# Two layers of graph attention on one core: in the sets of v product 6 goes ahead of product 3, and a block sum of features moves from VectorE to GpSimd

## The chip, the core and the metric

The kernel runs on one core of a Trainium2 chip. The metric is the device time of one execution in microseconds (us). Before the change three runs took 3329.23 to 3331.56 us, with a median of 3330.91 us.

The core has five engines that run their own instruction streams and wait for each other through semaphores: TensorE (PE in the profile; its weight loads are shown as PEld), VectorE (DVE), ScalarE (ACT), GpSimd (POOL) and SyncE (SP), which here only starts transfers.

## The reference

There are 4096 nodes with 512 features and an adjacency matrix of 4096 x 4096. Layer 0 is graph attention with 4 heads of 128, layer 1 is masked attention with 8 heads of 64; each is added to its input and normalised.

```python
x = _layernorm(x + _L0_gnn_ref(x, adj, ...), axis=-1)
x = _layernorm(x + _L1_gnn_ref(x, adj, Wks, Wqs, Wvs, Wo), axis=-1)

# in _L1_gnn_ref
adj = jnp.maximum(adjacency_matrix, eye)
q = jnp.einsum('nd,hdk->hnk', node_matrix, Wqs)
k = jnp.einsum('nd,hdk->hnk', node_matrix, Wks)
v = jnp.einsum('nd,hdk->hnk', node_matrix, Wvs)
scores = jnp.einsum('hqk,hmk->hqm', q, k) * kd ** (-0.5)
scores = scores + IDENTITY_BIAS * eye - MASK_VAL * (1.0 - adj)
att = jax.nn.softmax(scores, axis=-1)
return jnp.einsum('hqm,hmk,hko->qo', att, v, Wo)
```

The change lies in the three lines that make q, k and v: three matrix products of 4096 x 512 by 512 x 512, in float32.

## The kernel before

The program has four stages, one behind the other: the projections of layer 0 (to about 216 us of the span), its attention (to 1126 us), the projections q, k and v of layer 1 (to about 1412 us), and the attention of layer 1 with the output projection (to the end). The order of instructions on each engine is the order in which the Python code issues them.

**A set.** The features are taken in four pairs of 512-row groups (pair 0 to 3), that is 1024 rows at a time. For each pair `gemm` is called three times, for k, q and v: a set. A set treats the features (1024 x 512) and the weights (512 x 512) as two matrices of 2 x 2 blocks and makes the four blocks of the result, "11", "12", "21" and "22", from seven block products instead of eight. Products 1, 2, 3 and so on are numbered in the code; some of their factors are plain blocks, others are sums of blocks, made beforehand by `combine_weights` for weights and `combine_features` for features. The results follow from

- "11" = product 1 + product 2
- u2 = product 1 + product 6, and "12" = u2 + product 5 + product 3
- u2 becomes u2 + product 7, and "21" = u2 + product 4, "22" = u2 + product 5

The tile `u2` holds the running sum (two buffers), and `p5` holds product 5 (one buffer). An add with an operand in PSUM is on VectorE (`add`, L1283); the two adds of p5 read SBUF only and are on GpSimd (`pool`, L1277): first p5 into "12", called out12 below, later u2 + p5 into "22", called out22. Each finished block goes to device memory in two transfers on SyncE's queue (L1268, L1273). The text that follows uses the short names of the profile: v_sb and k_sb are the tiles for results, since `take_out` borrows them.

**Small sets.** From pair 1 on, some products are themselves made of seven small products of quarter size: products 1, 5, 6 and 7 in the k and q sets, products 1 and 5 in the v sets. `begin` issues four of them, `end` the other three (L1294 for v, L1298 for k and q), and a full product of something else stands between, so that VectorE and ScalarE have time to empty PSUM. These "deep" sets are issued by `in_parts` from a list, `plan`. A pair (1, 0) in it is the begin of product 1, (1, 1) its end, a plain number a whole product (L1248 for v, L1255 for k and q). The v set of pair 0 and the v set of pair 3 have no small sets and follow the older order 1, 5, 2, 6, 7, 3, 4; only the v sets of pairs 1 and 2 take the part of the list that the change edits. For brevity "(6, 0)" is also called the small set 6.

**PSUM.** `new` takes a tile of the pool of three s_ps tiles (1024 columns), `spread` takes both x_ps tiles (512 columns each), of which there are no more. In a deep v set products 2 and 3 are spread, and 1, 5, 6, 4 and 7 take new tiles in turn. A product can only start when the tile that it takes has been read.

**Sums for the next pair.** While a v set runs, the sums of features that the next pair needs are made: on VectorE four block sums of 128 x 1024 (`combine_features`, L1224) into the tiles x_s (products 5, 6 and 4) and in place (7), and on GpSimd quarter sums of 128 x 256, four for each small set 1, 5, 6 and 7 (`combine_features2`, L1214), into the tiles x2_s. They depend on each other: block sum 6 is made from 5, block sum 4 from 6, and the quarter sums of 5, 6 and 7 from the block sum of the same number. The tiles bear the name adjT in the profile, or xT for the sum in place. `beside_at(n, fn, ...)` puts such a step behind product n of the set: it is issued there, on its engine, behind the adds of that product.

Of the kernel before, what the change touches and what calls it, by code (L numbers as in the profile page):

```python
# [429 lines left out]
def tile_gat_then_masked_attention(  # L430
# [16 lines left out]
    nc = tc.nc  # L447
# [119 lines left out]
    with tc.tile_pool(name="l0", bufs=NG) as l0, \  # L567
# [77 lines left out]
        with tc.tile_pool(name="l0s", bufs=2) as sp:  # L645
# [264 lines left out]
            for g in range(NG):  # L910
                fs[g] = l0.tile([P, 2, GT, H0], F32, name="f")
                s4 = sp.tile([P, H0, GT, W0], F32, name="s4")
                plan = end if g == NG - 1 else usual if g else begin
# [60 lines left out]
        def turn_x1(g, n, c):  # L974
            nc.vector.transpose(
                xTs[g][:, c, n * HG:(n + 1) * HG].rearrange("p (b r) -> p b r", r=SQ),
                ys[g, n][:, :, c * SQ:(c + 1) * SQ])
# [119 lines left out]
    with wait_by_tile("l1", 1) as l1, wait_by_tile("l1a", 2) as lp, \  # L1097
# [46 lines left out]
        with wait_by_tile("l1s", 2) as sp:  # L1144
# [84 lines left out]
            def gemm(w, sums, kind, pair, beside, deep=()):  # L1229
# [7 lines left out]
                def new():  # L1237
                    return [ps.tile([P, HP, G], F32, name="s_ps").rearrange("p e r -> p (e r)")]
# [25 lines left out]
                def store(c, queue=nc.sync):  # L1264
                    for n in range(2):
                        m, g = 2 * (int(c[0]) - 1) + n, 2 * pair + int(c[1]) - 1
                        if kind == "v":
                            queue.dma_start(  # L1268
                                v_d[m][g // 2][:, g % 2 * GT:(g % 2 + 1) * GT, :],
                                out[c].rearrange("p (t d) -> p t d", t=GT)[  # L1270
                                    :, :, n * P:(n + 1) * P])
                        else:
                            queue.dma_start(k_d[m][g // 2][:, g % 2, :] if kind == "k"  # L1273
                                              else q_d[m][g], out[c][:, n * G:(n + 1) * G])

                def pool(dst, a, c, op):
                    nc.gpsimd.tensor_tensor(dst, a, c, op=op)  # L1277

                def add(dst, t):
                    n = 2 * G // len(t)  # L1280
                    for k, src in enumerate(t):
                        at = slice(k * n, (k + 1) * n)
                        nc.vector.tensor_tensor(dst[:, at], src, u2[:, at], op=ALU.add)  # L1283

                def spread():
                    return [xp.tile([P, GT, P], F32, name="x_ps").rearrange("p t r -> p (t r)")
                            for _ in range(2)]
# [66 lines left out]
                def results(i):  # L1354

                    if i == 1:
                        add(out["11"], held.pop(2))
                        store("11")
                    elif i == 6:
                        add(out["12"], held.pop(3))  # L1360
                        pool(out["12"], out["12"], p5, ALU.add)
                        later.at(1, lambda: store("12"))
                    elif i == 7:
                        pool(out["22"], u2, p5, ALU.add)
                        add(out["21"], held.pop(4))
                        store("21")
                        later.at(1, lambda: store("22"))

                def in_parts():
                    plan = [(1, 0), (5, 0), 2, (1, 1), (5, 1)]  # L1370
                    plan += [(6, 0), 3, (6, 1), (7, 0), 4, (7, 1)] if 6 in deep else [3, 6, 4, 7]
                    for i in plan:
                        if isinstance(i, int):
                            t = new() if i in (4, 6, 7) else spread()
                            product(i, t)
                            if i in (6, 7):
                                add(u2, t)
                                results(i)
                            else:
                                held[i] = t  # L1380
                        else:
                            i, phase = i
                            if phase == 0:
                                begin(i, p5 if i == 5 else u2, i in (1, 5))
                                continue
                            end(i)
                            results(i)
                        for fn in beside.get(i, []):
                            fn()
                        later.step()  # L1390

                if deep:
                    in_parts()
                    return
# [41 lines left out]
            for pair in range(NG // 2):  # L1436
                more = pair + 1 < NG // 2
                halves = [(2 * pair + 2 + n // 2, n % 2) for n in range(4)] if more else []

                def bring(n):  # L1440
                    load_x1(*halves[n], turn_p if pair % 2 else sp)

                def turn(n):
                    for c in range(KC):
                        turn_x1(*halves[n], c)

                beside = {}

                def beside_at(n, fn, *args):
                    beside.setdefault(n, []).append(lambda: fn(*args))  # L1450

                def parts(kind):
                    return inner[kind] if pair and (more or kind != "v") else ()

                if pair == 0:
                    combine_features(nc.vector, 0, 5)
                    for n, i in ((1, 6), (5, 7), (2, 3)):
                        beside_at(n, combine_weights, nc.vector, wk, wk_s, i)
                    for n, i in ((1, 6), (5, 7), (2, 4)):
                        beside_at(n, combine_features, nc.vector, 0, i)  # L1460
                    for i, n in ((5, 7), (6, 7), (7, 3), (3, 4)):
                        beside_at(n, combine_weights, nc.gpsimd, wq, wq_s, i)
                    beside_at(4, load_all, wv, wvs)
                elif pair == 1:
                    for n, i in ((2, 1), (5, 5), (3, 6), (4, 7)):
                        beside_at(n, combine_weights2, nc.vector, "q", wq, wq_s, i)
                if more:
                    for k, n in ((5, 0), (7, 1)):
                        beside_at(k, bring, n)
                gemm(wk, wk_s, "k", pair, beside, parts("k"))  # L1470
                beside = {}
                if pair == 0:
                    for i, n in ((5, 5), (6, 2), (7, 6), (3, 7)):
                        beside_at(n, combine_weights, nc.gpsimd, wv, wv_s, i)
                elif pair == 1:
                    for n, i in ((2, 1), (3, 5)):
                        beside_at(n, combine_weights2, nc.gpsimd, "v", wv, wv_s, i)
                if more:
                    for k, fn, n in (((2, turn, 0), (2, bring, 2), (4, turn, 1), (4, bring, 3),
                                      (7, turn, 2)) if pair else  # L1480
                                     ((1, turn, 0), (5, turn, 1), (5, bring, 2), (6, bring, 3),
                                      (4, turn, 2))):
                        beside_at(k, fn, n)
                else:
                    load_adjT(0, 0)
                    load_q(0, 0)
                gemm(wq, wq_s, "q", pair, beside, parts("q"))
                beside = {}
                if more:
                    beside_at(2 if pair else 1, turn, 3)  # L1490
                    if pair == 0:
                        for n, i in ((2, 1), (6, 5), (7, 6), (3, 7)):
                            beside_at(n, combine_weights2, nc.vector, "k", wk, wk_s, i)
                    for i, n in ((5, 5), (6, 6), (7, 3 if pair else 2), (4, 4)):
                        beside_at(n, combine_features, nc.vector, pair + 1, i)
                    for i, n in (((1, 1), (5, 6), (6, 4), (7, 7)) if pair else
                                 ((1, 1), (5, 6), (6, 3), (7, 4))):
                        beside_at(n, combine_features2, nc.gpsimd, pair + 1, i)
                else:
                    beside_at(5, load_kv, 0, 0, 0)  # L1500
                    beside_at(2, load_adjT, 0, 1)
                    for t in range(GT):
                        beside_at(2, finish_md, 0, t)
                    beside_at(7, load_kv, 0, 0, 1)
                    for c in range(2, NCJ):
                        beside_at(3, load_adjT, 0, c)
                gemm(wv, wv_s, "v", pair, beside, parts("v"))
                xTs.pop(2 * pair)
                xTs.pop(2 * pair + 1)
# [280 lines left out]
```

## Time and profile before

| what | us |
| --- | --- |
| median of three runs | 3330.91 |
| the profiled execution | 3330.41 |
| its span | 3328.3 |
| TensorE busy | 3301.2 |
| VectorE busy | 2484.2 |
| GpSimd busy | 2167.3 |
| v set of pair 1, first matmul to first matmul of the next set | 24.56 |
| v set of pair 2, the same | 24.56 |

The span runs from the first instruction to the last of the profiled execution; its own time is longer by what lies around it. The page gives the busy time of each engine. A wait is given as the idle time of an engine and what ended it: "<-DVE p L1311" means that an instruction of line 1311 on VectorE, writing p, did. In timelines a row is a group of equal instructions with its start, its length, the engine, the line, the tiles out<-in, the shape and the count. One matmul of the code can be two rows' worth of records (a product of eight matmuls is "x16" in the v sets). In the table by stage each row has the stretch, its length, and the busy times of the engines in the order PE, PEld, DVE, ACT and POOL, each with its count, then the clock of TensorE as a share, the share of the transfer engines and GB/s.

### The profile page before, as it was taken

The page shows a single profiled execution, that of the slowest core. Times are in us where ns is not written, and L with a number is a line of the kernel's source. Part 1 is how long each engine was busy: PE and PEld are TensorE (multiplying, and loading weights), DVE is VectorE, ACT ScalarE, POOL GpSimd, SP SyncE. Part 2 cuts the span into 40 slices and gives each one's busy share as a digit, 9 for nine tenths or more (in the row PEclk, how much of TensorE's full clock was granted, in tenths as well). Part 3 has the DMA queues.
Part 4 walks back from the last instruction along what each step waited for, and adds up shares of the span by engine and source line. Part 5 has one row for each costly group of instructions (what it writes and reads, how often), then busy time and mean ns, then how long its engine had stood idle before and what let it go on. Part 6 is the DMA issues. An engine that isn't in the chain of part 4 may idle for free.

```text
span 3328.3 us, 67210 instructions
## 1 busy us (share of the span) xinstructions
PE 3301.2 (99%) x27160; PEld 1965.5 (59%) x27160; DVE 2484.2 (75%) x3189; ACT 1949.1 (59%) x2439; POOL 2167.3 (65%) x1599
## 2 busy tenths in 40 slices
PE   9999999999999999999999999999999999999998
PEld 8899999999999777733333333333333333333333
DVE  6789899899999676567767676676766767667676
ACT  1267868878776310156656556566565656656554
POOL 5630040040030243389999999999999999999996
PEclk9999999999999999999999999999999999999999
DMA  8988796686532443489888988879888799887984
GB/s 180 227 204 183 219 187 169 152 184 146 137 93 58 111 149 114 149 223 205 191 211 226 224 202 191 210 188 257 203 194 212 186 214 244 194 210 186 213 196 112
DMA packets 398992, 612.04 MB, mean 184 GB/s; under 512 B 167632, under 2 KB 248528, under 8 KB 398672
## 3 DMA queue, kind: packets, MB, share of 16 engines
q0 software_dynamic: 97520, 258.77, 42.6%
q1 hardware_dynamic: 299280, 345.88, 33.5%
q8 instruction: 215, 3.52, 0.4%
q10 hardware_dynamic: 1872, 3.02, 0.4%
q14 instruction: 105, 0.86, 0.1%
HBM read 315.87 MB, written 109.25 MB: 128 GB/s over the span
## 4 chain that ended last, share of the span: by engine, by line
PE 92%; POOL 3%; DMA 2%; DVE 1%; issue 1%; ACT 0%; ACTq 0%; POOLq 0%; DVEq 0%
PE o_ps L1087 27%; PE o_ps L1597 24%; PE s_ps L1138 24%; PE o_ps L846 5%; PE s_ps L1661 3%; PE s_ps L1298 2%; PE s_ps L1255 2%; DMA p<-p 2%; PE s_ps L1248 1%; PE x_ps L1255 1%; POOL q_sum L1572 1%; PE x_ps L1248 1%; PE s_ps L1616 1%; POOL p L1582 0%; POOL adjT L1214 0%
## 5 line engine op out<-in xcount | busy, mean ns | idle before, releaser
L1572 POOL TENSOR_TENSOR q_sum<-q_sum,p 128x1024 f32<-128x1024 f32 x538 | 1378.0, 2561 | 64.0 <-DMA p<-p 38.2
L1552 DVE TENSOR_TENSOR p<-s_ps,adjT 128x1024 f32<-128x1024 f32 x896 | 1043.9, 1217 | 470.1 <-ACT s_ps L1549 438.4
L1549 ACT ACTIVATE s_ps<-s_ps 128x1024 f32<-128x1024 f32 x1021 | 967.5, 1006 | 597.3 <-PE s_ps L1138 594.2
L1138 PE MATMUL s_ps<-q_sb,k_sb 64*64 64x512 f32 x8192 | 943.5, 589 | 2.8 <-DVE p L1552 2.7
L1597 PE MATMUL o_ps<-p,v_sb 64*64 64x512 f32 x8192 | 943.6, 590 | 0.0
L1087 PE MATMUL o_ps<-sup_t,p 128*128 128x129 f32 x8192 | 915.7, 275 | 1.2 <-DVE p L640 1.2
L1087 PEld LDWEIGHTS o_ps<-sup_t,p 128*128 128x128 f32 x8192 | 915.3, 192 | 1.7 <-DVE p L640 1.4
L640 DVE SCALAR_TENSOR_TENSOR p<-fr_t,dj,az 128x1024 f32<-128x1024 f32 x512 | 650.2, 1284 | 66.1 <-PE o_ps L1087 37.9
L1138 PEld LDWEIGHTS s_ps<-q_sb,k_sb 64*64 64x64 f32 x8192 | 312.4, 133 | 569.9 <-issue 453.7
L1597 PEld LDWEIGHTS o_ps<-p,v_sb 64*64 64x64 f32 x8192 | 310.2, 133 | 570.7 <-issue 560.4
L624 ACT ACTIVATE z<-fr_t,f 128x1024 fp8e4<-128x1024 f32 x512 | 557.9, 1146 | 102.1 <-DVE az L635 101.8
L1582 POOL DMA_DIRECT2D p<-p x412 | 438.4, 1302 | 10.1 <-PE o_ps L1597 9.2
L1063 POOL DMA_DIRECT2D agg<-base_d x32 | 29.1, 1217 | 386.8 <-DMA sup_t<-sup_d 204.7
L585 POOL COPY seen<-token 128x1 f32<-128x1 f32 x24 | 10.9, 455 | 356.8 <-DVE token L583 356.8
L1552 DVE TENSOR_TENSOR p<-s_ps,md 128x1024 f32<-128x1024 f32 x128 | 150.8, 1218 | 67.0 <-ACT s_ps L1549 63.6
L635 DVE TENSOR_TENSOR az<-adjT,z 128x512 int32<-128x512 int32 x256 | 175.4, 685 | 2.9 <-ACT z L624 1.8
L600 ACT ACTIVATE adjT<-stage 128x1024 fp8e4<-128x1024 bf16 x128 | 131.2, 1055 | 17.0 <-DMA stage<-adj_d 16.7
L1661 PE MATMUL s_ps<-wo_sb,on 128*128 128x512 f32 x240 | 110.8, 604 | 0.0
L1631 ACT ACTIVATE r<-r_h 32x256 f32<-32x256 f32 x248 | 102.3, 413 | 2.9
L1277 POOL TENSOR_TENSOR v_sb<-v_sb,p 128x1024 f32<-128x1024 f32 x8 | 20.6, 2569 | 95.9 <-DVE v_sb L1283 52.4
L1049 ACT ACTIVATE agg<-o_ps,rinv 128x128 f32<-128x128 f32 x128 | 42.0, 370 | 69.8 <-DVE den L1042 45.9
L1322 ACT ACTIVATE v<-s_ps 128x256 f32<-128x256 f32 x28 | 10.8, 384 | 117.6 <-PE s_ps L1298 102.5
(274 smaller groups left out, 2257.3 us busy)
## 6 DMA issues: line engine op xcount, KB each, us to landing
p<-p POOLq DMA_DIRECT2D x412, 512.0 KB, 9.1
k_sb<-k_d SPq DMA_DIRECT2D x128, 512.0 KB
v_sb<-v_d SPq DMA_DIRECT2D x128, 512.0 KB
adj_d<-in_adj_dram POOLq DMA_DIRECT2D x32, 1024.0 KB, 11.0
sup_t<-sup_d SPq DMA_DIRECT2D x120, 258.0 KB
fr_t<-fr_d SPq DMA_DIRECT2D x16, 1024.0 KB
adjT_d<-adjT SPq DMA_DIRECT2D x32, 512.0 KB
adjT<-adjT_d SPq DMA_DIRECT2D x32, 512.0 KB
```

The lines of the kernel that those rows point to most:

```text
L624: nc.scalar.activation(z[:, k, :], fr_t[w, h][:, 0, :], AF.Sign, bias=fs[j // GT][:, 0, (j + k) % GT, h:h + 1], saturate=False)
L635: nc.vector.tensor_tensor(az.bitcast(I32), adjT[w, j // CJ][:, j % CJ:j % CJ + 2, :].bitcast(I32), z.bitcast(I32), op=ALU.bitwise_and)
L640: nc.vector.scalar_tensor_tensor(p, fr[:, 1, :], dj[j // GT][:, j % GT, h:h + 1], az_t[w, h, j // 2][:, j % 2, :], op0=ALU.max, op1=ALU.mult)
L846: nc.tensor.matmul(out[:, t * HD:(t + 1) * HD], xb[:, c, t * P:(t + 1) * P], wb[:, c, :], start=not more and t == 0 and c == 0, stop=c == ...
L1087: nc.tensor.matmul(o[t // BK][:, t % BK, :], p[:, t * P:(t + 1) * P], s, start=(j == 0 and t % BK == 0), stop=(j == NT - 1), skip_group_ch ...
L1138: nc.tensor.matmul(s[c:c + MS, e, :], k[r, a + c:a + c + MS], qt[g, m][r, :], start=True, stop=True)
L1549: nc.scalar.activation(s, s, AF.Exp, scale=float(KD) ** -0.5)
L1552: nc.vector.tensor_tensor(p, s, keep[:, None, :].to_broadcast([P, HP, G]), op=ALU.mult)
L1572: nc.gpsimd.tensor_tensor(q, q, p, op=ALU.add)
L1582: later.at(2, lambda: nc.gpsimd.dma_start(a, b, accum_op=ALU.add))
L1597: nc.tensor.matmul(o[c, n, :], v[r, j % CH, c], p[r, e, :], start=(j == 0), stop=(j == NT - 1))
L1661: nc.tensor.matmul(s, on_t[g][:, m, t * P:(t + 1) * P], wo_sb[:, m, :], start=(m == 0), stop=(m == NP1 - 1))
```

## The change

Three edits. First, in the deep v sets (pairs 1 and 2) product 6 is issued ahead of product 3; the adds for "12" now stand behind product 3, and those for "21" and "22" behind product 7, as before. Second, GpSimd's quarter sums are ordered anew: in the v set of pair 0 those of 7 ahead of those of 6; in the v sets of pairs 1 and 2 those of 7 come behind product 3 and those of 6 behind product 7, where before they stood the other way round behind products 4 and 7. With that GpSimd has the quarter sums of 5 ahead of out12, and those of 7 between out12 and out22; those of 6 follow out22. Third, block sum 4 (128 x 1024) is no longer issued on VectorE behind product 4 but on GpSimd, as its last step of the set.

On VectorE the block sum of 7 comes behind the adds of "12" now, because product 3 is later in the list.

```diff
                 def in_parts():
                     plan = [(1, 0), (5, 0), 2, (1, 1), (5, 1)]
-                    plan += [(6, 0), 3, (6, 1), (7, 0), 4, (7, 1)] if 6 in deep else [3, 6, 4, 7]
+                    plan += [(6, 0), 3, (6, 1), (7, 0), 4, (7, 1)] if 6 in deep else [6, 3, 4, 7]
                     for i in plan:
                         if isinstance(i, int):
                             t = new() if i in (4, 6, 7) else spread()
                             product(i, t)
                             if i in (6, 7):
                                 add(u2, t)
-                                results(i)
                             else:
                                 held[i] = t
+                            if i == 7 or i == 3 and 6 not in deep:
+                                results(2 * i if i == 3 else i)
...
-                    for i, n in ((5, 5), (6, 6), (7, 3 if pair else 2), (4, 4)):
+                    for i, n in ((5, 5), (6, 6), (7, 3 if pair else 2)):
                         beside_at(n, combine_features, nc.vector, pair + 1, i)
-                    for i, n in (((1, 1), (5, 6), (6, 4), (7, 7)) if pair else
-                                 ((1, 1), (5, 6), (6, 3), (7, 4))):
+                    for i, n in (((1, 1), (5, 6), (7, 3), (6, 7)) if pair else
+                                 ((1, 1), (5, 6), (7, 7), (6, 4))):
                         beside_at(n, combine_features2, nc.gpsimd, pair + 1, i)
+                    beside_at(7 if pair else 4, combine_features, nc.gpsimd, pair + 1, 4)
```

## The prediction

> **What bounds the kernel now.** I read the page first, then the list of what TensorE waited for, then the chain that ended last around the sets of v, then the timelines there.
>
> The page:
>
> ```profile
> span 3328.3 us, 67210 instructions
> ...
> PE 3301.2 (99%) x27160; PEld 1965.5 (59%) x27160; DVE 2484.2 (75%) x3189; ACT 1949.1 (59%) x2439; POOL 2167.3 (65%) x1599
> ...
> PE 92%; POOL 3%; DMA 2%; DVE 1%; issue 1%; ACT 0%; ACTq 0%; POOLq 0%; DVEq 0%
> ```
>
> TensorE is busy for 99% and carries 92% of the chain. Work that leaves VectorE or GpSimd is worth only what TensorE waits for it. The list of TensorE's waits (total us, times, longest) has two rows from the sets that the change edits:
>
> ```profile
> PE s_ps L1138 <- DVE p L1552: 2.7, 3, 1.8
> PE s_ps L1298 <- DVE p L1311: 1.8, 2, 0.9
> PE x_ps L1248 <- DVE v_sb L1283: 1.6, 2, 0.8
> ```
>
> The lower two come once in the v set of each of the second and third pairs of feature blocks, and in the k set behind it. TensorE's timeline around the first (start, length, in brackets the idle time before):
>
> ```profile
> 1252.67 0.61 PE L1294 MATMUL s_ps<-wv_s,adjT 128*128 128x128 f32 x4
> 1254.08 3.69 PE L1248 MATMUL x_ps<-adjT,xT 128*128 128x256 f32 x16 [0.80 <-DVE v_sb L1283]
> 1257.61 3.62 PE L1248 MATMUL s_ps<-wv_s,adjT 128*128 128x256 f32 x16
> ...
> 1275.72 0.59 PE L1298 MATMUL s_ps<-adjT,wk 128*128 128x256 f32 x2
> 1277.23 0.67 PE L1298 MATMUL s_ps<-adjT,wk_low 128*128 128x256 f32 x2 [0.92 <-DVE p L1311]
> ```
>
> At 1254.08 product 3 waits: it writes the two x_ps tiles that held product 2, and VectorE empties them until 1254.53. At 1277.23, in the next k set, the end of small set 5 waits for VectorE's p, which waits for GpSimd. The chain names what GpSimd did:
>
> ```profile
> 1263.94 3.20 POOL v_sb L1277
> 1267.14 1.67 POOL adjT L1214
> ...
> 1273.85 2.32 POOL k_sb L1277
> 1276.17 0.02 issue
> 1276.20 0.44 DVE p L1311
> ```
>
> Between out12 (v_sb, from 1263.94) and out22 (k_sb, from 1273.81) stand eight quarter sums of the next pair's features (L1214). p5 has one buffer, so the k set can't write it until out22 has read it. Both engines were slow beside each other here; two of VectorE's block sums (L1224) and one quarter sum, from the two engines' timelines:
>
> ```profile
> 1263.72 4.50 DVE L1224 TENSOR_TENSOR adjT<-xT,adjT 128x1024 f32<-128x1024 f32 x2
> ...
> 1267.11 1.71 POOL L1214 TENSOR_TENSOR adjT<-adjT 128x256 f32<-128x256 f32 x1
> ```
>
> Alone, the first kind takes 1.22 each and the second 0.73. Busy time by stage (length, then PE) puts a size on the waits; the rows are the k set without a wait, the v set, and the k set behind it:
>
> ```profile
> 1198.34:1220.90 22.56, 22.56 (x81) 15.11 (x80) 18.88 (x43) 2.20 (x6) 6.42 (x6) 1.00 0.38 114
> 1243.41:1267.97 24.56, 23.76 (x138) 21.53 (x137) 18.88 (x30) 1.54 (x4) 9.24 (x7) 1.00 0.32 99
> 1267.97:1291.50 23.53, 22.61 (x81) 15.11 (x80) 14.28 (x25) 2.31 (x6) 13.17 (x14) 1.00 0.41 121
> ```
>
> **The skill.** The Trainium skill, "GPSIMD Engine Reference", section 8 (Key points), says that GpSimd shares its SBUF interfaces with VectorE and contends with VectorE's instructions that have two SBUF inputs. The trace agrees: 4.50 for two sums against 2.44, 3.20 for out12 against 2.36, 1.71 against 0.73; sums that read PSUM beside GpSimd stay at 1.23. Section 3.1 of that page measures an elementwise add on GpSimd 1.96 times as long as on VectorE; here 2.36 against 1.22 is 1.93. "Perfetto Trace Analysis", "Tensor Engine Instruction", says that TensorE's end times are modelled; so I take losses from start to start, and here the idle of 0.80 indeed understates its loss.
>
> **The change, part by part.**
>
> *Loss of a pair now.* The groups of small matmuls in front step by 0.445 (the group before began at 1252.22), so product 3 was due at 1253.12 and lost 0.96; its own steps to the next product are 3.53 where the others take 3.45, another 0.08. That is 1.04. For the k set, 23.53 less 22.56 is 0.97.
>
> *Product 6 ahead of 3 (second and third v set).* Product 6 writes an s_ps tile that was free since 1245.9 and reads sums made a set earlier: it starts at 1253.12. Product 3 follows at 1256.57, 2.0 after the x_ps tiles are empty. Product 4 (1260.03) and 7 (1263.48) wait for ScalarE's copies that end at 1253.20 and 1255.70. The set ends at 1266.94. Matmuls are neither added nor removed: 1.04 gained.
>
> *The adds that move with it.* VectorE: sum of 5 until 1256.33; u2 with product 6 at 1256.8 to 1258.0; sum of 6 until 1259.3 alone, 1261.2 if contended as above (3.18); out12 until 1262.5; sum of 7 until 1263.7, contended 1265.7; u2 with product 7 at 1267.1 to 1268.4; out21 to 1269.6. All fits in front of product 7's end, as VectorE idled 3.68 here before.
>
> *GpSimd's order.* Quarter sums of 5 from 1256.36 (4 x 0.73 = 2.9, and 2 more for two contended ones): 1261.2. out12 from 1262.5, 3.20: 1265.7. Quarter sums of 7: 1268.6. out22 then, 2.36: 1271.0 instead of 1276.1. VectorE wants p5 about then, finishes its two p adds (2 x 0.44) by 1272.0, and the end part of small set 5 is due at 1275.11 (1266.94 + 2 x 1.73 + 3.43 + 1.29). The wait is gone with 3.1 to spare: 0.97 gained.
>
> *What is late next.* Quarter sums of 6 now stand behind out22: 1271.0 to 1273.9. The first is read in the k set at 1276.8 (small set 6 begins at 1276.4, its second block 0.43 later): 5.1 to spare. The fourth block sum, moved from VectorE, is not shown on GpSimd; the nearest row is out22's add of the same shape, 2.36, and contended 3.20, both ends of the bound. It ends at 1276.3 to 1277.1; product 4 of that k set reads it at 1284.6. Its 1.22 (3.18 contended) leave VectorE, where it hid in TensorE's products: worth nothing by itself.
>
> *First pair's v set.* This set has no parts and keeps its order of products, and TensorE waits for none of it. GpSimd does the quarter sums of 7, then of 6, from 1195.3 to 1202.5, then the fourth sum to 1205.7 at worst. They are read at 1207.8 and 1216.2. Zero; without that cover, each us late costs one us.
>
> *SyncE, other queues.* No transfer is added or moved past another. Stores of out12 and out22 leave earlier (1265.7 and 1271.0 for 1267.2 and 1276.2).
>
> *Sum.* Two pairs x (1.04 + 0.97) = 4.0; adding a delay of about 0.1 that only the k set without a wait has (its product 3 takes 3.53 to the next start, not 3.43), 4.2 at most. I take 4.1. The profiled execution took 3330.4, 2.1 around its span of 3328.3: 3326.3 with a span of 3324.2. The median of the three runs is 0.5 higher: 3330.9 - 4.1 = 3326.8. What follows is bound by TensorE, so the time gained should arrive whole.
>
> **The rivals.**
>
> *Slower: GpSimd is late for the small sets.* If every GpSimd instruction of the stretch ran at its contended price (1.71 and 3.20), the sums of 5 end at 1263.2, out12 at 1266.4, sums of 7 at 1273.3, out22 at 1276.5. The p adds then let the end part of small set 5 start at 1277.5, 2.4 late, and small set 6 waits 1.5 for its second and third sums (1279.9, 1281.6). Against the 2.0 removed, 1.9 lost per pair: 3334.7. The wait returns when out22 ends after 1274.0, and the pair is slower than before from about 1274.5, with those 1.5 behind it. Against it: only one of eight quarter sums was contended before, and VectorE has two such sums here of 1.22.
>
> *Only the wait for x_ps goes.* If contention makes out22 about 5 late, the k set keeps its wait of 0.97 and the gain is 2 x 1.04: 3328.8. For it: the price of contention depends on alignment that the trace shows only once per pair.
>
> *Nothing arrives.* The attention stage after it has TensorE waits of 2.7 in all, fed by accumulating transfers of 13 to 16 us on the chain; shifted by 4, they may fall elsewhere and take the gain: 3331. The same waits gone would give 3324.1. Against both: 2.7 in some 1900 us is little.
>
> **How the numbers follow.** Both waits gone 0.68 (3325.5 to 3328); only one 0.11; nothing arrives 0.10; slower 0.05; both gone and attention's waits too 0.06. The range takes the first two and half of each neighbour: 3324.4 to 3330.0. About 0.2% (6.7 us) is what a measurement of this kernel can tell from no change; the gain I forecast is 0.12%. Faster than that needs 3324.2 or less: 0.05. Slower needs 3337.6: beyond even the rival's price, 0.02. Within: 0.93.
>
> **What would show it.** Right: TensorE's waits have neither the x_ps row of 1.6 nor the s_ps row of 1.8; deep v sets take 23.5 instead of 24.6 and the k sets behind them 22.5 instead of 23.5; out22 ends some 4 ahead of the end part of small set 5. Wrong: a wait of L1298 or L1255 for GpSimd's adjT, or a quarter sum mean far above 0.9; or those sets shortened and the span not, which would point to the attention stage. A new wait at product 6, which I hold to be free, would void the first part.

## The result, and the profile after

The changed kernel takes 3325.71 us in the median (3324.33 to 3329.80, 22 runs), the kernel before 3330.28 (3327.04 to 3332.60, 22 runs beside them). The ratio is 0.9987, with a 95% interval of 0.9981 to 0.9993: 4.57 us less, a difference that the interval keeps apart from none, but smaller than the 0.2% that the prediction took as its bound. The forecast was 3326.8, 4.1 below the median shown then. The profiled execution took 3324.41.

The page of the kernel after; the last line gives the shares of the chain that ended last:

```profile
span 3322.5 us, 67217 instructions
...
PE 97%; DVE 1%; DMA 1%; POOL 1%; issue 0%; ACT 0%; ACTq 0%; POOLq 0%; DVEq 0%
```

TensorE carries 97% of the chain where it carried 92%, and GpSimd 1% instead of 3%. Little of that is the change: e1 below, which has neither of the two waits, still shows 92% and 3%, and 4 us are 0.12% of the span. The rest lies in the attention stage: transfers (DMA p<-p) have 2.3% of the chain in e1, one piece of 13.97 us in this execution. Which of its waits end up in the chain differs from one execution to the next. The list of TensorE's waits is sorted by total, and its top is now

```profile
PE o_ps L846 <- ACT z L863: 3.4, 1, 3.4
PE o_ps L886 <- POOL ident masks.py:199: 1.4, 1, 1.4
PE o_ps L1087 <- DVE p L640: 1.2, 1, 1.2
```

The row of L1298 (1.8 before) and that of L1248 (1.6 before) would stand between the first two of these. Both are gone, as forecast; the attention's row of 2.7 (L1138) is gone too, of which more below.

Where the time left shows best in the lengths of the sets, each from its first matmul to the first of the next set (us):

| kernel | k, pair 1 | v, pair 1 | k, pair 2 | v, pair 2 | k, pair 3 |
| --- | --- | --- | --- | --- | --- |
| before | 22.56 | 24.56 | 23.54 | 24.56 | 23.54 |
| after | 22.56 | 23.52 | 22.52 | 23.52 | 22.52 |

Twice 1.04 in the v sets and twice 1.02 in the k sets behind them: 4.12. Two rows of the table by stage, the v set of pair 1 and the k set behind it (stretch, length, then the busy times of PE, PEld, DVE, ACT and POOL, clock, share of the transfer engines, GB/s):

```profile
1244.25:1267.77 23.52, 23.52 (x138) 21.45 (x137) 15.86 (x29) 1.54 (x4) 14.92 (x14) 1.00 0.39 124
1267.77:1290.29 22.52, 22.52 (x81) 15.11 (x80) 14.17 (x24) 2.20 (x6) 10.00 (x8) 1.00 0.35 105
```

TensorE is busy for the whole of both. Before, it was busy for 23.76 of 24.56 and 22.61 of 23.53. TensorE's timeline in the same two sets:

```profile
1253.95 3.62 PE L1248 MATMUL s_ps<-wv_s,adjT 128*128 128x256 f32 x16
1257.41 3.62 PE L1248 MATMUL x_ps<-adjT,xT 128*128 128x256 f32 x16
...
1275.95 0.59 PE L1298 MATMUL s_ps<-adjT,wk_low 128*128 128x256 f32 x2
```

Product 6 (s_ps) comes first, product 3 (x_ps) 3.46 behind it, and neither row, nor the end part of small set 5 at 1275.95, has a bracket with idle time. GpSimd's timeline:

```profile
1258.74 1.81 POOL L1214 TENSOR_TENSOR adjT<-adjT 128x256 f32<-128x256 f32 x1
...
1261.89 3.21 POOL L1277 TENSOR_TENSOR v_sb<-v_sb,p 128x1024 f32<-128x1024 f32 x1 [0.65 <-issue]
...
1269.27 2.36 POOL L1277 TENSOR_TENSOR k_sb<-u,p 128x1024 f32<-128x1024 f32 x1 [1.32 <-DVE u L1283]
...
1274.45 2.36 POOL L1224 TENSOR_TENSOR adjT<-xT,adjT 128x1024 f32<-128x1024 f32 x1
```

The stage begins 0.84 later in this execution: the first product of its first set starts at 1126.94, before at 1126.10. The change does not touch what makes this difference. It is there when layer 0's attention starts (chain: 216.90, before 216.05), and that attention takes 910.2 in both. In the projections ahead of it TensorE's granted clock is at half behind an early wait, from 12.83 to 19.66 us here and from 14.87 to 18.29 before. With the 0.84 taken off, out22 ends at 1270.8, where before it ended at 1276.2, and VectorE's second p add ends at 1273.25 of the profile's time, 2.7 before the small set needs it (1275.95). Block sum 4, the last row, is new on GpSimd and takes 2.36.

In the profiled executions the span fell by 5.8, more than the median. The account: 4.12 in the sets; 2.5 between the first matmul of pair 3's q set and the end (1966.19 before, 1963.66 after), where TensorE's two waits in attention went from 2.7 and 0.3 to 0 and 0.5; less the 0.84. The attention's wait is no effect of the change. In the profiled executions of the experiments, which change nothing there, it was 2.3, 1.5, 2.2, 2.7, 3.1, 2.3, 2.1, 2.4, 1.6 and 1.0 (in the order e1, e2, e3, e4, e5, e6a, e6b, e7, e8a, e8b); so the 0 of the changed kernel is at the low end of what executions differ by.

The start of the stage differs in the same way. Four of the kernels below (e4, e7, e8a, e8b) have no stretch at half clock in layer 0's projections and begin the stage at 1123.96 to 1124.41; those with one stretch of 3.41 us begin it at 1125.47 to 1126.48. So of the kernels with one execution only the lengths of the sets are compared, not the times.

### The profile page after: what moved, and what is told of

The parts are those of the page before. It is cut to its first block, busy times and chain, and to the rows that moved or that the text cites. A ratio compares the mean times of both kernels' runs of the same rounds, so it can differ in the third digit from the quotient of the medians.

```text
span 3322.5 us, 67217 instructions
## 1 busy us (share of the span) xinstructions
PE 3301.6 (99%) x27160; PEld 1967.0 (59%) x27160; DVE 2477.7 (75%) x3186; ACT 1947.7 (59%) x2439; POOL 2173.3 (65%) x1602
## 3 DMA queue, kind: packets, MB, share of 16 engines
q10 hardware_dynamic: 1872, 3.02, 0.4%
## 4 chain that ended last, share of the span: by engine, by line
PE 97%; DVE 1%; DMA 1%; POOL 1%; issue 0%; ACT 0%; ACTq 0%; POOLq 0%; DVEq 0%
PE o_ps L1087 27%; PE o_ps L1599 26%; PE s_ps L1138 26%; PE o_ps L846 5%; PE s_ps L1663 3%; PE s_ps L1298 2%; PE s_ps L1248 2%; PE s_ps L1255 2%; PE x_ps L1255 1%; PE x_ps L1248 1%; PE s_ps L1618 1%; DMA p<-p 0%; PE s_ps L1294 0%; DMA w_sb<-in_L_gnn_weight_dram 0%; DVE p L1731 0%
## 5 line engine op out<-in xcount | busy, mean ns | idle before, releaser
L1138 PE MATMUL s_ps<-q_sb,k_sb 64*64 64x512 f32 x8192 | 942.9, 589 | 0.1
L1138 PEld LDWEIGHTS s_ps<-q_sb,k_sb 64*64 64x64 f32 x8192 | 312.6, 133 | 566.4 <-issue 453.9
L1663 PEld LDWEIGHTS s_ps<-wo_sb,on 128*128 128x128 f32 x240 | 43.3, 189 | 55.9 <-issue 55.7
```

Source lines behind the costliest of these rows:

```text
L1138: nc.tensor.matmul(s[c:c + MS, e, :], k[r, a + c:a + c + MS], qt[g, m][r, :], start=True, stop=True)
L1663: nc.tensor.matmul(s, on_t[g][:, m, t * P:(t + 1) * P], wo_sb[:, m, :], start=(m == 0), stop=(m == NP1 - 1))
```

## The experiments

The prediction put the 1.04 of the v set to product 6, and the 0.97 of the k set to GpSimd's new order. The rival theory was that the order of the products does both: where product 6 precedes product 3, "12" is finished later, so that out12 falls behind the quarter sums of 5 without any edit on GpSimd. The expectations below call the first theory A and this rival B; theory C is that a lighter VectorE, without block sum 4, brings the gain. The prediction held that move to be worth nothing by itself.

### e1: the order of the products alone

GpSimd's order and block sum 4 stay as before the change.

```diff
-                    plan += [...] if 6 in deep else [3, 6, 4, 7]
+                    plan += [...] if 6 in deep else [6, 3, 4, 7]
...
-                                results(i)
...
+                            if i == 7 or i == 3 and 6 not in deep:
+                                results(2 * i if i == 3 else i)
```

> Product 6 ahead of 3 alone; GpSimd's order behind its products and block sum 4 on VectorE stay as before. Theory A (two separate waits, one freed by each part of the change): the v sets of pairs 1 and 2 fall from 24.56 to 23.52, the k sets behind them stay at 23.5; 2.1 us faster than before. Theory B (the order of products does it all, because the quarter sums of 5 stand behind product 6 and so move ahead of out12 by themselves, which leaves only four between out12 and out22): v sets 23.52 and k sets 22.55, 4.1 us faster, as the whole change. Theory C (a lighter VectorE brings the gain): v sets 23.52 at best, out12 and out22 as late as before, k sets 23.5. I take B.

Measured: 3324.96 us (3322.42 to 3327.75, 21 runs) against 3329.32 of the kernel before (41 runs), a ratio of 0.9988 (0.9981 to 0.9995). The five sets take 22.56, 23.52, 22.53, 23.52, 22.52: both waits are gone. GpSimd's timeline of this kernel:

```profile
1261.43 3.21 POOL L1277 TENSOR_TENSOR v_sb<-v_sb,p 128x1024 f32<-128x1024 f32 x1 [0.75 <-issue]
1264.59 1.71 POOL L1214 TENSOR_TENSOR adjT<-adjT 128x256 f32<-128x256 f32 x1
...
1268.82 2.36 POOL L1277 TENSOR_TENSOR k_sb<-u,p 128x1024 f32<-128x1024 f32 x1 [0.34 <-DVE u L1283]
```

Only four quarter sums (those of 6) stand between out12 and out22 here, since those of 5 ran at 1256.79 to 1260.68, ahead of out12. So out22 starts at 1268.82 and is bounded by VectorE's u2, not by GpSimd's list. Theory B was right: the order of the products alone gives both gains. VectorE has all its work here, so theory C is not needed.

### e2: GpSimd's order and block sum 4, without the order of the products

```diff
-                    for i, n in ((5, 5), (6, 6), (7, 3 if pair else 2), (4, 4)):
+                    for i, n in ((5, 5), (6, 6), (7, 3 if pair else 2)):
...
-                    for i, n in (((1, 1), (5, 6), (6, 4), (7, 7)) if pair else
-                                 ((1, 1), (5, 6), (6, 3), (7, 4))):
+                    for i, n in (((1, 1), (5, 6), (7, 3), (6, 7)) if pair else
+                                 ((1, 1), (5, 6), (7, 7), (6, 4))):
...
+                    beside_at(7 if pair else 4, combine_features, nc.gpsimd, pair + 1, 4)
```

> GpSimd's new order and block sum 4 on GpSimd, but product 3 ahead of product 6 as before. Theories A and B: the wait for x_ps stays (v sets 24.56), the wait for p5 is gone (k sets 22.55); 2.0 us faster than before. Theory C: the same, so this run does not part C from them; but if the wait for x_ps goes too, then a lighter VectorE is its cause, and C holds.

Measured: 3327.07 (3324.68 to 3332.17, 21 runs), a ratio of 0.9993 (0.9987 to 1.0000) to the same runs of before. The sets take 22.56, 24.56, 22.53, 24.56, 22.53. TensorE's list of waits has no row of L1298, and keeps

```profile
PE x_ps L1248 <- DVE v_sb L1283: 1.6, 2, 0.8
```

GpSimd's edits remove the k sets' wait (2 x 1.01), and the v sets' wait stays to the hundredth. That is half of the gain, where e1 alone has all of it: the k sets' half is bought twice.

### e3 and e4: each half of GpSimd's edits

e3 moves block sum 4 alone, and e4 changes the quarter sums' order alone.

```diff
# e3
-                    for i, n in ((5, 5), (6, 6), (7, 3 if pair else 2), (4, 4)):
+                    for i, n in ((5, 5), (6, 6), (7, 3 if pair else 2)):
...
+                    beside_at(7 if pair else 4, combine_features, nc.gpsimd, pair + 1, 4)
# e4
-                    for i, n in (((1, 1), (5, 6), (6, 4), (7, 7)) if pair else
-                                 ((1, 1), (5, 6), (6, 3), (7, 4))):
+                    for i, n in (((1, 1), (5, 6), (7, 3), (6, 7)) if pair else
+                                 ((1, 1), (5, 6), (7, 7), (6, 4))):
```

> Block sum 4 on GpSimd as its last step of the set, everything else as before (eight quarter sums between out12 and out22). Theory A: out22 still stands behind eight quarter sums; it is about 1 us earlier since none of them waits for VectorE's block sum 4, so the wait for p5 shrinks from 0.97 to 0.1 or 0.2 (k sets 22.7), v sets 24.56. If contention were no cause, k sets stay at 23.5. Theory C (lighter VectorE is the gain): k sets 22.55, no wait left, and v sets shorter than 24.56 as well.

> GpSimd's quarter sums in the new order alone; block sum 4 on VectorE and product 3 ahead of 6 as before. Theory A: only the four quarter sums of 5 stand between out12 and out22, those of 7 come in front; out22 ends about 3 us earlier than before, the wait for p5 is gone: k sets 22.55, v sets 24.56; about 2 us faster. Theory C: VectorE has all its work, so nothing is gained: k sets 23.5.

Measured, one execution each, so that the sets tell more than the times: e3 3327.88, e4 3326.26. Both have v sets of 24.55 to 24.56, and k sets behind them of 22.56 (e3) and 22.53 (e4). Either edit alone removes the k sets' wait.

For e4 that was expected: its out22 starts at 1268.81. For e3 I had expected 22.7. The 22.56 is what theory C named for the k sets, but the v sets that C would shorten stay at 24.56. Two rows of e3, GpSimd's out22 and VectorE's first p add:

```profile
1273.15 2.35 POOL L1277 TENSOR_TENSOR k_sb<-u,p 128x1024 f32<-128x1024 f32 x1
...
1275.53 0.43 DVE L1311 TENSOR_TENSOR p<-s_ps,v 128x256 f32<-128x256 f32 x1 [2.76 <-POOL k_sb L1277]
```

All eight quarter sums still stand between out12 and out22. But without VectorE's block sum 4 beside it, the first of them takes 0.73 instead of 1.71. Counted from the start of the k set (1268.28 here, 1267.97 before), out22 ends 7.22 into it, where it ended at 8.20: 1.0 earlier. VectorE still waits for it, 2.76, and the end part of small set 5 begins 0.10 late (1276.56; the step to it is 0.53 instead of 0.43), of which the whole set shows 0.04. The wait before the change was just as long as one quarter sum was held up.

### e5: two buffers for p5

Here the kernel before keeps its orders, and p5 gets a second buffer, which is taken from v2.

```diff
-                u2, p5 = (... for n, b in (("u2", 2), ("p5", 1)))
+                u2, p5 = (... for n, b in (("u2", 2), ("p5", 2)))
...
-                    v2 = sp.tile([P, HG], F32, name="v2", bufs=3)
+                    v2 = sp.tile([P, HG], F32, name="v2", bufs=2)
```

> The kernel before with a second buffer for p5 (and two in place of three for v2, to make room). If the wait in the k sets is for the one buffer of p5, which out22 still reads, then k sets fall from 23.54 to 22.55 while GpSimd stays as late as before (out22 ends some 9 us behind out12) and v sets stay at 24.56. If the wait is for anything else that comes late with GpSimd, k sets stay at 23.5.

Measured: 3328.97 in one execution. The k sets behind v take 22.50, the v sets 24.58. Of this kernel, out22 and the first p add again:

```profile
1273.92 2.35 POOL L1277 TENSOR_TENSOR k_sb<-u,p 128x1024 f32<-128x1024 f32 x1
...
1272.60 0.42 DVE L1311 TENSOR_TENSOR p<-s_ps,v 128x256 f32<-128x256 f32 x1
```

GpSimd is as late as before the change (out22 ends 8.19 into the k set, before 8.20), and the p add runs 1.3 before out22 even starts. So what TensorE waited for was the one p5 buffer, and not GpSimd's lateness as such. Nothing else in this k set waited for out22.

### e6a, e8a, e8b, e6b: how late GpSimd may be, and what it costs

The slower rival of the prediction needs GpSimd to be late. Four kernels make it so: in the changed kernel the quarter sums of 7 are computed again, into the same tiles with the same values, ahead of out22: once (e6a), twice (e8a), twice and a half (e8b) or three times (e6b) more. Each further time is 4 instructions, some 2.8 us.

```diff
+                    for _ in range(N if pair else 0):
+                        beside_at(4, combine_features2, nc.gpsimd, pair + 1, 7)
# N: 1 in e6a, 2 in e8a and e8b, 3 in e6b; e8b has further
-            def combine_features2(engine, pair, i):
-                for k in (5, 6, 7, 4):
+            def combine_features2(engine, pair, i, ks=(5, 6, 7, 4)):
+                for k in ks:
...
+                    if pair:
+                        beside_at(4, combine_features2, nc.gpsimd, pair + 1, 7, (5, 6))
```

> The changed kernel with the four quarter sums of 7 made once more between out12 and out22 (2.9 us of GpSimd). By the account of spare time out22 ends about 1.5 later than in the changed kernel (1.3 of the 2.9 fit into GpSimd's idle time there), small set 5 has about 1.6 to spare yet: v sets 23.52, k sets 22.53, no time lost. If GpSimd had become the bound, the k sets take 1.5 longer each.

> The changed kernel with the four quarter sums of 7 made twice more between out12 and out22: 2.9 less of GpSimd than with three repeats, where the end part of small set 5 began 3.9 late. So it begins 1.1 late. If the extra loss of 2.4 that the run with three repeats had came from TensorE's clock, which fell to half behind its long wait, a wait of 1.1 leaves the clock at 1.00 and the k sets take 22.53 + 1.1 = 23.6. If a late start costs more than itself whatever its length (other waits behind it), the k sets take 24 or more.

> As with two repeats, and two quarter sums more (1.5 us): the end part of small set 5 begins 2.5 late. If the clock holds through a wait of 2.5, the k sets take 22.53 + 2.5 = 25.0 with a clock of 1.00; if it falls already here, they take about 27 and the clock behind the wait shows 0.50.

> The changed kernel with the four quarter sums of 7 made three times more between out12 and out22 (8.6 us of GpSimd): the rival in which GpSimd is late, made true. The last of them ends 8.6 behind the end of the first quarter sums of 7, out22 2.36 after that, VectorE's p adds 1.03 later: the end part of small set 5 comes 4.0 late in each of two k sets. K sets 26.6, v sets 23.52, about 8 us slower than the changed kernel and 3.7 slower than before. If a late out22 can hide elsewhere, the k sets take clearly less than 26.6.

Measured (e6b has 15 runs, before and after 22 each, and the others one execution each, whose times say little; the v sets take 23.52 in all four):

| kernel | time | out22 ends, into the k set of pair 2 | TensorE's wait at L1298 | k, pair 2 | k, pair 3 | lost in each k set |
| --- | --- | --- | --- | --- | --- | --- |
| after | 3325.71 | 3.86 | none | 22.52 | 22.52 | |
| e6a | 3326.88 | 5.37 | none | 22.53 | 22.53 | 0.0, 0.0 |
| e3, from above | 3327.88 | 7.22 | none listed | 22.56 | 22.56 | 0.0, 0.0 |
| before | 3330.28 | 8.20 | 0.9, 0.9 | 23.54 | 23.54 | 1.0, 1.0 |
| e8a | 3325.71 | 8.21 | 0.93, 0.92 | 23.55 | 23.55 | 1.0, 1.0 |
| e8b | 3329.62 | 9.71 | 2.42, 2.40 | 25.05 | 26.68 | 2.5, 4.2 |
| e6b | 3337.96 | 11.04 | 3.75, 3.76 | 28.97 | 29.02 | 6.5, 6.5 |

For e6b the runs of before beside it have a median of 3330.66, and the ratio is 1.0021 (1.0013 to 1.0029), 7.3 slower where 3.7 was expected: the mechanism of the slower rival exists, and it does end on the other side.

e8a brings out22 back to where it was before the change, to 0.01, and with it the wait of before and its loss: that is the k set's half of the change run backwards on the changed kernel. Its TensorE timeline:

```profile
1274.33 0.67 PE L1298 MATMUL s_ps<-adjT,wk_low 128*128 128x256 f32 x2 [0.93 <-DVE p L1311]
1274.84 0.59 PE L1298 MATMUL s_ps<-adjT,w_sk 128*128 128x256 f32 x2
```

The wait sets in where out22 ends 7.1 to 7.2 into the k set (e3), so the changed kernel has 3.3 of slack there. The prediction's point, 1274.0 with the set starting at 1266.94, was 7.1. Up to e8a a lateness costs its own length. e6b missed its expectation of 26.6 by 2.4 in each set. TensorE's timeline of e6b around the wait:

```profile
1278.39 1.19 PE L1298 MATMUL s_ps<-adjT,wk_low 128*128 128x256 f32 x2 [3.75 <-DVE p L1311]
1279.37 1.06 PE L1298 MATMUL s_ps<-adjT,w_sk 128*128 128x256 f32 x2
...
1283.64 0.60 PE L1298 MATMUL s_ps<-adjT,adjT 128*128 128x256 f32 x2
```

Pairs of matmuls that take 0.59 in the changed kernel take 1.06 behind the wait, until 1283.64. The granted clock in the table by stage is 0.85 in 1274 to 1278, 0.50 in 1278 to 1280, and 1.00 again from 1284. From the end part's first matmul to the next whole product it is 5.69, where the changed kernel has 3.02: 2.67 in addition to the wait of 3.75, together 6.4 of the 6.5.

e8b shows where that begins. Its two k sets wait equally long, and only one of them pays:

```profile
1276.00 0.67 PE L1298 MATMUL s_ps<-adjT,wk_low 128*128 128x256 f32 x2 [2.42 <-DVE p L1311]
1276.51 0.59 PE L1298 MATMUL s_ps<-adjT,w_sk 128*128 128x256 f32 x2
...
1347.05 1.19 PE L1298 MATMUL s_ps<-adjT,wk_low 128*128 128x256 f32 x2 [2.40 <-DVE p L1311]
1348.04 1.06 PE L1298 MATMUL s_ps<-adjT,w_sk 128*128 128x256 f32 x2
```

The table by stage has a clock of 1.00 behind the first and 0.50 behind the second (1347.00 to 1348.50). The first set lost 2.5 for its 2.42, the second 4.2 for its 2.40. Why only one of them pays is worked out in the last section.

### e7: block sum 4 back on VectorE

The changed kernel, with the sum where it was before.

```diff
-                    for i, n in ((5, 5), (6, 6), (7, 3 if pair else 2)):
+                    for i, n in ((5, 5), (6, 6), (7, 3 if pair else 2), (4, 4)):
...
-                    beside_at(7 if pair else 4, combine_features, nc.gpsimd, pair + 1, 4)
```

> The changed kernel with block sum 4 back on VectorE behind product 4. Nothing of it is on the path: v sets 23.52, k sets 22.53, no time lost. It also tells how VectorE and GpSimd disturb each other: if they take turns (the later one waits for the whole instruction of the other), block sum 4 or the add beside it takes its own time plus what was left of the other (block sum 4 about 1.8, then GpSimd's next quarter sum about 1.8), and the rest stays at 1.22, 2.36 and 0.73; if they share, both are stretched at once while they overlap.

Measured: 3323.93 in one execution, sets of 22.56, 23.52, 22.53, 23.52, 22.53. With the rest of the change in place, moving the sum is worth nothing. VectorE's sum in this kernel:

```profile
1261.88 1.67 DVE L1224 TENSOR_TENSOR adjT<-xT,adjT 128x1024 f32<-128x1024 f32 x1 [1.63 <-PE s_ps L1248]
```

It takes 1.67 beside GpSimd, and VectorE idles before and after it. GpSimd's next quarter sum takes 1.71. Both are near the 1.8 that the expectation gave for taking turns (more in the last section); out12, which it held at 2.36, took 3.21, as in the changed kernel. Its time is a single execution 1.8 below the median of the changed kernel, whose own executions spread over 5.5 (3324.33 to 3329.80), and the sets are the same to 0.01; the stage begins 2.6 earlier (1124.31), with no stretch at half clock ahead of it. Nothing here shows a version that beats the changed kernel.

## Why the prediction was right

**The size.** Forecast: 1.04 and 0.97 per pair, 4.1 in all. Measured: 1.04 and 1.02, 4.12 in the sets and 4.57 in the medians. The 0.05 beyond the 0.97 is about half of the 0.1 that the sum left open as "4.2 at most": the k sets after take 22.52, 0.04 less than the one that had no wait before (22.56).

**The order on TensorE.** Product 6 was placed at 1253.12, product 3 at 1256.57 and the small set's end part at 1275.11. They came at 1253.95, 1257.41 and 1275.95, each 0.83 to 0.84 later, which is by how much the stage began later. Product 6 is free at its place, as held.

**GpSimd's list.** out22 was to end at 1271.0 and ended at 1270.8 (less the 0.84). That this fits so well is partly luck: the quarter sums of 7 in front of it were to end at 1268.6 and ended at 1267.1, and out22 then stood 1.32 for VectorE's u2, whose end the prediction had at 1268.4. So VectorE set its start, and not GpSimd's list. Behind it, the quarter sums of 6 were to end at 1273.9 and ended at 1273.7; block sum 4 took the lower end of its bound, 2.36. The end of the p adds was forecast at 1272.0 and came at 1272.4, because VectorE's adds of small set 5, not GpSimd, were the last to allow it: 2.7 to spare instead of 3.1. Either is far from zero, and e6a, which makes out22 1.5 later against its set, loses nothing.

**The first pair's v set.** Zero was forecast. From the first product of pair 0's k set to the first matmul of pair 1's it is 72.24 in both kernels.

**What was not right, with the sum untouched.** The prediction credits GpSimd's order with the 0.97 ("Quarter sums of 5 from 1256.36 ... out12 from 1262.5 ... The wait is gone"). e1 shows that this step is not needed. The late "12" of the new product order puts the quarter sums of 5 ahead of out12 by itself, and that is enough. The prediction had the times for that (the sums of 5 possible from 1256.36, the last add of "12" by 1262.5) and did not ask which edit caused it. Either of the two GpSimd edits also suffices (e3, e4). The wait was small, and three edits each remove it, so the sum of the parts measured alone (4.1 from e1, 2.0 from e2) is more than the whole.

**Contention.** The prediction gave VectorE's block sums of 6 and 7 up to 3.18 each (1258.0 to 1261.2, and 1262.5 to 1265.7). Neither was held up in the changed kernel; both took 1.22, and GpSimd took the delay (its 1.81 and 3.21 above). In e1, e6b, e8a and e8b the sum of 6 took 1.78 to 1.79, so this can fall either way. In the changed kernel:

```profile
1258.75 1.22 DVE L1224 TENSOR_TENSOR adjT<-xT,adjT 128x1024 f32<-128x1024 f32 x1
...
1261.67 1.22 DVE L1224 TENSOR_TENSOR xT<-xT 128x1024 f32<-128x1024 f32 x1
```

**The rivals.** The slower one had its mechanism right and its price made up wrongly. For a set that is 2.4 late it put 3.9 (2.4, and 1.5 for small set 6; 1.9 per pair after the 2.0 removed), which adds up waits only. e8b has that lateness and lost 2.5 once and 4.2 once. The 1.5 did not come (the quarter sums took 0.73 there and not 1.71, so its condition was not met); what did come, once, was 1.7 from the clock, which the sum lacked. Where its wait sets in was right, as the table shows, but not that a pair is slower than before from 1274.5: e8a is beyond that point (8.21 into the set, 1275.15 on the prediction's scale) and loses 1.0 of the 2.0 gained. "Only the wait for x_ps goes" is what e8a looks like, with out22 4.35 later than in the changed kernel; contention added nothing near that. "Nothing arrives" pointed at the attention's waits. They vary from 0 to 3.1 from execution to execution, so they can hide or add most of a gain of 4 in a single pair of profiled executions (5.8 here); between the medians of 22 runs each, 4.57 was left.

## What to carry to other kernels

When several edits come together, ask of each wait which edit alone would remove it, from the times already in the profile: a wait of 1 us behind a late add can be removed by several edits, and their gains don't add up. Where the bound engine waits for a buffer, a second buffer of the same tile (e5) tells cheaply whether the buffer or the late producer is the cause. Price a rival's wait on TensorE as more than its length once it comes to 2 us, because the matmuls behind it may run at half speed, and work out the slack in front of it in us (here 3.3) before trusting a plan.

## What the runs showed of the hardware

**VectorE and GpSimd take turns by whole instructions.** The prediction treated contention as both engines being slowed. The rows fit another reading: where both have an add or sum whose two inputs lie in SBUF, the one that comes second gets no further than its first 0.15 us or so until the other is done. In the changed kernel GpSimd's quarter sum at 1258.74 took 1.81: VectorE's sum ran 1258.75 to 1259.97, and the quarter sum, 0.73 alone, ended 0.58 after it. (Its recorded start is 0.01 ahead of VectorE's, so the recorded starts don't say who goes first when they are that close.) out12 at 1261.89 took 3.21: VectorE's sum of 7 ended at 1262.89 and out12 2.21 later, near its 2.36 alone. It goes the other way too. From e7, GpSimd's timeline beside VectorE's 1.67 shown above:

```profile
1259.26 3.21 POOL L1277 TENSOR_TENSOR v_sb<-v_sb,p 128x1024 f32<-128x1024 f32 x1 [0.65 <-issue]
...
1262.43 1.71 POOL L1214 TENSOR_TENSOR adjT<-xT 128x256 f32<-128x256 f32 x1
```

out12 took its 3.21 here because VectorE's sum of 7 ran until 1260.26, and ended 2.21 after that, at 1262.47. VectorE's sum 4, in hand since 1261.88, ends 1.08 after that, at 1263.55; GpSimd's next quarter sum, begun at 1262.43, ends 0.59 after that. The 3.18 before the change was of this kind: that sum began at 1265.04 and stood until out12 ended at 1267.14. The Trainium skill, "GPSIMD Engine Reference", section 8 (Key points), has the shared SBUF interfaces and the condition of two SBUF inputs; the trace agrees with both, since VectorE's adds that read PSUM took 0.41 to 0.42 each while out22 ran (three of them, from 1270.37 to 1271.70), as they do without it. An equal sharing while both run would have stretched both: VectorE's sum of 7 in e7 kept its 1.22 though out12 ran beside it for 1.0 of them. That the two take turns is read from such starts and ends; e7 expected about 1.8 for each of its two, and no other run was made for it. It means that the price is what is left of the other engine's instruction, 0.45 to 2 us in these rows, rather than a fixed factor.

**TensorE's clock fell after waits shorter than a window of the skill.** The Trainium skill, "TensorE: Matmul & The Clock Gate", Part 1 (The HAM clock gate), says that the clock goes to half after at least one idle window of about 3.4 us, and that the windows run freely. The waits of e6b are longer than that, 3.75 and 3.76, and the trace agrees: behind them the matmul pairs took 1.06 for 0.59, at a cost of about 2.7 each time. e8b differs: a wait of 2.40 had the same effect (1.06, clock 0.50) and a wait of 2.42 in the same execution had none. A start-to-start reading of the former leaves at most 2.57 without matmul (1347.05 less 1344.05, less 0.43), still under 3.4. Waits of 0.92 and 0.93 (e8a) had no such effect.

The traces settle where the windows lay. In each trace the granted clock changes only at moments that lie whole multiples of 3.41 us apart. In e6b, for example, it falls at 1276.82 and 1351.92 and is back at 1283.65 and 1358.74. Such steps counted back from the fall in e8b, at 1346.98, give the stretches that its two waits fell into (columns as before: stretch, length, busy times, clock):

```profile
1271.89:1275.31 3.42, 1.69 (x7) 0.95 (x5) 0.34 (x1) 0.00 (x0) 3.40 (x3) 1.00 0.00 0
1275.31:1278.72 3.41, 2.72 (x13) 2.44 (x14) 2.92 (x6) 0.38 (x1) 3.33 (x5) 1.00 0.58 184
1343.57:1346.98 3.41, 1.08 (x5) 0.60 (x4) 0.92 (x3) 0.00 (x0) 3.33 (x4) 1.00 0.01 3
1346.98:1350.40 3.42, 3.35 (x8) 2.75 (x9) 2.22 (x4) 0.38 (x1) 3.42 (x4) 0.50 0.75 249
```

The first wait was split between two stretches: TensorE stood 1.73 in one and 0.69 in the next. The second lay almost whole in one, 2.33 of 3.41, and the clock was at half for the stretch that followed, which cost the 1.7 (in e6b it was at half for two, 6.83). Over the twelve traces, from the clock's first rise to the last matmul, the clock fell behind every stretch in which TensorE stood for 2.05 or more (11 stretches; the least is 9.42 to 12.83 of the changed kernel) and behind none in which it stood for 1.95 or less (the most is 12.38 to 15.79 of e8b). The page's wording asks for a whole idle window; here some 2 us of one were enough, and the measurement decides. Its free-running windows agree with the trace. By these figures a wait up to 1.9 us leaves the clock alone, and one from about 4.1 us (twice 2.05, an estimate) lowers it wherever it falls; between the two it depends on where the stretches lie, which the kernel does not choose.
